# Two attention blocks in fp32: layer 0's V by Strassen twice over in all seven products, and the softmax sums inside it in two parts

## The chip, the cores and the metric

The kernel runs on one core of one Trainium2 chip. The metric is the time of one execution on the device in microseconds; lower is better. A core has TensorE (PE, matrix products), VectorE (DVE), ScalarE (ACT), GpSimd (POOL) and SyncE (SP), each with a stream of instructions of its own that it takes in order. SP and ACT also issue the DMAs here.

## The reference, cut to what matters

Eight samples of 512 channels by 1024 positions go through two attention blocks, everything in fp32.

```python
def _L0_conv_ref(x, norm_w, norm_b, qkv_w, qkv_b, proj_w, proj_b):   # 8 heads of 64 channels
    h = group_norm(x, norm_w, norm_b)
    qkv = jnp.einsum('oc,bchw->bohw', qkv_w, h) + qkv_b[None, :, None, None]
    ...
    attn = jax.nn.softmax(jnp.einsum('bhnd,bhmd->bhnm', q, k) * scale, axis=-1)
    o = jnp.einsum('bhnm,bhmd->bhnd', attn, v)
    ...
    return x + jnp.einsum('oc,bchw->bohw', proj_w, o) + proj_b[None, :, None, None]

def _L1_conv_ref(x, gn_gamma, gn_beta, wq, bq, wk, bk, wv, bv, wo, bo):   # one head of 512 channels
    ...
```

The change is in V of layer 0: a 512x512 weight times 512 channels by 1024 positions, for one sample.

## The kernel before, in words

**Strassen.** Each such product is cut 2x2 and made as seven products instead of eight: of the weight's parts `A11, A12, A22, S1` to `S4` and the sample's parts `B11, B21, B22, T1` to `T4`. `S` and `T` are sums and differences of quarters. The seven are kept in `PAIRS` (A12 B21, S1 T1, S4 B22, A22 T4) and `REST` (A11 B11, S2 T2, S3 T3). A "second step" makes each of the seven again by seven smaller ones. `make_twice` makes the weight's smaller sums once, in sample 0's attention, and stores them in DRAM; `WeightTwice` loads them from ACT's queue; `quarters_in_steps` makes the sample's, three DVE instructions for each part.

**Samples and stages.** While sample b is in layer 0's attention, nothing of b + 1 but its norm and its parts is made. Then `middle` makes, in this order: V of sample b + 1, the first half of its Q and K (the QK stage), the projection of sample b, and the second half of Q and K. Layer 1 of sample b follows, then attention of b + 1. `Kept` stores V, Q and K in DRAM meanwhile. There are seven such middles. Sample 0's own V is made in another way (`make_v`).

**V before.** `make_v_twice` calls `by_two_steps`: the four products of `PAIRS` by a second step (generator `pair`, two products side by side in a PSUM bank, each small product two matmuls of 128 columns), then the three of `REST` in one step (generator `line`, matmuls of 256 columns). Seven small products use two banks in turn: `line`, in which A11 B11, S2 T2, S3 T3 and A22 T4 are added up and read off after each, and `single`. Each is read off by ACT (`nc.scalar.copy`, the first to write a place) or by DVE (an add onto it).

**Banks.** Tags `s` and `o` have two PSUM buffers each of two banks, taken in turn. A group's `line` is an `s`, its `single` an `o`. So a stage's first products wait until the same buffers of the stage before are read off. `spares` holds the unused second banks, and `room(name, n)` gives the n-th.

**Softmax sums inside V.** The last two pairs of heads (the last "couple") end with attention. `fold` moves half of their sums over keys by DMA, `folded` adds them on DVE, `sum_couple` adds over partitions on PE with `ones` (eight matmuls of 64 rows by 32 columns), `copy_couple` copies to SBUF on ACT, and the rest is a chain of DMAs and one reciprocal:

```python
def one_over_couple(couple, queues):
    nc.vector.reciprocal(few, few)
    ...
    nc.sync.dma_start(rows.rearrange("m (a c) -> (m a) c", c=32), few)      # inv_rows <- few
    ...
            queues[j].dma_start(flat(spreads[pair])[j * HD : (j + 1) * HD], ...)   # inv <- inv_rows
```

In V `queues` are SP and ACT. `held_couple` is a short ACT instruction on `few`; `divide_at` (DVE) divides the attention's output `o` by the sums in the QK stage, and POOL halves the result for the projection.

**The order.** It is written out by hand: a generator yields after each small product, and `at_steps` runs the hooks of step n after it. `combine2` (T1 to T4 of `o`, on DVE), the fold, the sums and loads are such hooks in V. In attention, `ahead_steps` and `at_units` do the same by units; a unit is 1.716 us of PE (four score and four value matmuls). SBUF tiles come from one pool of 36 buffers (`tile2`), so that a new tile may wait for an old one.

**Where seven products by two steps stand already.** Layer 1's Q (`make_q_twice`) uses `seven_by_two_steps`: four groups z (A11 B11 and S2 T2), w (S3 T3 alone), c (S1 T1, A22 T4) and d (A12 B21, S4 B22), interleaved, first "zzwzwzwzwzwzww", then "ccdcdcdcdcdc", `exchange(0)`, "d", "d", `exchange(1)`.

Of the kernel before, what the change touches and what calls it, by code (L numbers as in the profile page):

```python
# [39 lines left out]
ALU = mybir.AluOpType  # L40
# [25 lines left out]
def two_attention_blocks(  # L66
# [488 lines left out]
    PAIRS_Q = [[("A12", "B21"), ("S4", "B22")], [("S1", "T1"), ("A22", "T4")]]  # L555
    PAIRS = [[("A12", "B21"), ("S1", "T1")], [("S4", "B22"), ("A22", "T4")]]
    REST = [[("A11", "B11"), ("S2", "T2")], [("S3", "T3")]]
    TWICE = {"wqk1": PAIRS + REST}

    class WeightTwice:  # L560

# [120 lines left out]
        yield from together(pair(0), pair(1))  # L682
        yield from together(line(0), line(1))

    def seven_by_two_steps(multiply, at, z, c, w, bias, name):

        def group(tag, products, use_of):
            line, single = (banks(t, f"ps_{t}{tag}_{name}") for t in "so")
            spares.extend([single[:, 1, :], line[:, 1, :]])
            line, single = line[:, 0, :], single[:, 0, :]
            for bank, x, y, start, fresh, r, t in [
                (line, "A11", "B11", True, True, 0, 0), (single, "A12", "B21", True, False, 0, 0),
                (line, "S2", "T2", False, True, 0, 1), (single, "S1", "T1", True, True, 1, 1),  # L700
                (line, "S3", "T3", False, False, 1, 1), (single, "S4", "B22", False, False, 0, 1),
                (line, "A22", "T4", False, True, 1, 0),
            ]:
# [24 lines left out]
        for k in range(2):  # L728
            plus(z[k][:, 1, :], z[k][:, 0, :], z[k][:, 1, :], bias and bias(k, 0))
        for k in range(2):  # L730
            plus(w[k], w[k], z[k][:, 1, :], bias and bias(k, 1))
        spares.clear()
        c_of, d_of = [("S1", "T1"), ("A22", "T4")], [("A12", "B21"), ("S4", "B22")]
        second = dict(c=group("c", c_of, (c, False)), d=group("d", d_of, (z, True)))

        def exchange(k):
            plus(z[k][:, 1, :], z[k][:, 1, :], c[k][:, 0, :])
            both = w[k].unsqueeze(1).to_broadcast([P, 2, HALF])
            nc.gpsimd.tensor_tensor(c[k], c[k], both, ALU.add)
# [266 lines left out]
    class Kept:  # L1006


        def __init__(self, pairs, name):
            self.name, self.n = name, [len(p) for p in pairs]  # L1010
            tiles = [flat(t) for p in pairs for t in p]
            self.rows = dram.tile([P, len(tiles) * N], FP, tag=f"kept_{name}", name=f"kept_{name}")
            for n, t in enumerate(tiles):
                nc.sync.dma_start(self.rows[:, n * N : (n + 1) * N], t)

        def back(self):
            n, pairs = 0, []
            for size in self.n:
                pairs.append([])
                for _ in range(size):  # L1020
                    pairs[-1].append(tile2(f"{self.name}_back_{n}"))
                    nc.sync.dma_start(flat(pairs[-1][-1]), self.rows[:, n * N : (n + 1) * N])
                    n += 1
            return pairs

    def pairs_qk_twice(w, twice_a, oc, bs, twice_b, pairs, b):

# [128 lines left out]
    def layer0(bs, qs, ks, vs, b, norm_next, ending, begun):  # L1156
# [69 lines left out]
        if b == 0:  # L1226
# [16 lines left out]
            hooks[7].append(p0.finish)  # L1243
            at_steps(together(*pairs_qk(w, 1, bs, qs, ks, b)), hooks)
            steps = []
            for name, ns in [("v0", range(2)), ("p0", range(2)), ("wqk1", range(4))]:
                of = [columns_of(of) for of in waiting if of.name == name]
                steps += make_twice(name, ns, of[0] if of else None, early=not of)
            for n, step in enumerate(steps):
# [50 lines left out]

        couples, folds, ps_couple = [ORDER[:2], ORDER[2:]], {}, []

        def fold(pair):

# [12 lines left out]
        def sum_couple(couple, banks_of):  # L1319


            for n, (pair, j) in enumerate((pair, j) for pair in couple for j in range(2)):
                for g, bank in enumerate(banks_of):
                    rows = slice(g * HD, (g + 1) * HD)
                    nc.tensor.matmul(
                        bank[n * 32 : (n + 1) * 32, :], ones[rows, :32], accs[pair, 0][rows, j, :],
                        start=True, stop=True,
                    )
            ps_couple[:] = banks_of

        def copy_couple(couple, g):
            if g == 0:
# [34 lines left out]
        def couple_steps(i):  # L1367
            if ended(i - 1) is not None:
                fold(ended(i - 1))
            if ended(i - 5) is not None:  # L1370
                folded(ended(i - 5))
            couple = couples[0]
            if ended(i - 7) == couple[1]:
                ps_sum = banks("o", f"ps_sum_{b}_{couple[0]}")
                sum_couple(couple, [ps_sum[:, g, :] for g in range(2)])
# [8 lines left out]
        ahead_a, ahead_b, ahead = [], {}, {}  # L1384

        def ahead_steps(i):
            if i == 44:
                for part in ["B21", "T1", "B22", "T4"]:
                    ahead_b[part], steps = quarters_in_steps(
                        combine.parts[part], tile2(f"{part}_twice_0_{b + 1}_0")  # L1390
                    )
                    for step in steps:
                        ahead[45 + len(ahead)] = step
# [112 lines left out]
    def middle(b, bs, twice_w, twice_b, comb, combine2, bias, hooks_v, divisions):  # L1506
# [1 line left out]


        to, comb_twice, xs = {"qs": [None] * NC, "ks": [None] * NC}, {}, []  # L1510
        v_pairs = places_v(f"0_{b + 1}")
        hooks_v.setdefault(8, []).append(lambda: twice_w.append(WeightTwice("qk02")))
        at_steps(
            make_v_twice(next_weight("v0"), twice_w.pop(0), bs, twice_b, v_pairs, f"v_0_{b + 1}"), hooks_v
        )
# [6 lines left out]
        hooks = {n: [division] for n, division in enumerate(divisions)}  # L1522
        for n in range(1, 5):
            hooks[2 * n + 3] = [lambda n=n: combine2(n, 1)]
        for n, part in [(3, "B21"), (3, "B22"), (5, "T1"), (11, "T4")]:
# [1161 lines left out]
```

## Time and profile before

| what | value |
|---|---|
| time, median of 3 runs | 2778.61 us (2778.32 to 2780.92) |
| the profiled execution's own time | 2779.2 us |
| its span in the profile | 2777.5 us |
| one V stage, first product to QK's first | 24.24 us, in each of the seven |
| QK stage after it | 22.39 us |
| attention of layer 0 (samples 0 to 6) | 110.35 us |
| granted TensorE clock | full throughout |

"Busy" on PE runs from a matmul's start to its modelled end; matmuls overlap, so the pace is read from start to start. An fp32 matmul leaves two records. "Idle before, releaser" names what ended an engine's idle time. In lists by order of time the columns are start, duration (both us), engine, line, operation, output and inputs, shapes, count.

### The profile page before, as it was taken

How to read it: one execution, taken by the hardware profiler on the slowest of the kernel's cores; microseconds unless marked ns; L12 is line 12 of the kernel's file. 1: busy time of each engine (PE TensorE's matmuls, PEld its weight loads, DVE VectorE, ACT ScalarE, POOL GpSimd, SP SyncE). 2: the span in 40 equal slices, each digit the busy share in tenths (PEclk: the TensorE clock that was granted, in tenths of full speed). 3: DMA queues.
4: the chain of work that ended last, by engine and by line, in shares of the span. 5: the costliest groups of instructions: out<-in, count | busy, mean ns of one | idle time of the engine just before them, and what ended most of it. 6: DMA issues, size and time to landing. Idle time of an engine off the chain costs nothing.

```text
span 2777.5 us, 41752 instructions
## 1 busy us (share of the span) xinstructions
PE 2769.1 (100%) x16318; PEld 1646.7 (59%) x16318; DVE 2137.0 (77%) x3023; ACT 1186.8 (43%) x1911; POOL 589.4 (21%) x612
## 2 busy tenths in 40 slices
PE   9999999999999999999999999999999999999999
PEld 5437764377643786447764477645676356853375
DVE  6797777877778777887778776887768877688877
ACT  3462533625346153462525525265342643226621
POOL 0001440015400253002530044300432005220121
PEclk9999999999999999999999999999999999999999
DMA  7545514265142652326432263322633236241101
GB/s 257 202 135 199 200 57 141 59 210 184 57 141 59 213 182 80 122 62 231 156 120 82 77 227 145 136 74 73 239 129 140 69 101 239 71 171 32 35 16 40
DMA packets 114527, 358.62 MB, mean 129 GB/s; under 512 B 25052, under 2 KB 25852, under 8 KB 107920
## 3 DMA queue, kind: packets, MB, share of 16 engines
q1 hardware_dynamic: 89856, 299.68, 31.6%
q10 hardware_dynamic: 24464, 56.16, 6.2%
q8 instruction: 131, 2.15, 0.3%
q14 instruction: 76, 0.62, 0.1%
HBM read 252.77 MB, written 79.21 MB: 120 GB/s over the span
## 4 chain that ended last, share of the span: by engine, by line
PE 96%; DVE 2%; DMA 1%; ACT 1%; issue 0%; SPq 0%; POOL 0%; ACTq 0%; POOLq 0%
PE ps_o L1195 16%; PE s L1146 16%; PE ps_o L2005 10%; PE ps_l_qk L1044 5%; PE ps_l L1837 5%; PE ps_l_v L793 5%; PE ps_s L1820 4%; PE ps_s L1837 4%; PE ps_s_qk L1037 3%; PE ps_s_v L1065 3%; PE ps_o_qk L1037 3%; PE ps_l_p L778 3%; PE ps_o_v L1065 2%; PE ps_s_two L2135 2%; PE ps_s_p L1102 2%; PE ps_o_two L2135 1%
## 5 line engine op out<-in xcount | busy, mean ns | idle before, releaser
L950 ACT ACTIVATE p<-s 128x1024 f32<-128x1024 f32 x505 | 516.4, 1024 | 308.6 <-PE s L1146 301.1
L952 DVE TENSOR_TENSOR acc<-acc,p 128x1024 f32<-128x1024 f32 x384 | 468.6, 1220 | 63.6 <-ACT p L950 54.9
L1146 PE MATMUL s<-qk_back,qk_back 64*64 64x512 f32 x3528 | 457.4, 590 | 0.0
L1195 PE MATMUL ps_o<-p,v_back 64*64 64x512 f32 x3528 | 455.3, 589 | 0.0
L1195 PEld LDWEIGHTS ps_o<-p,v_back 64*64 64x64 f32 x3528 | 134.9, 133 | 243.6 <-issue 239.8
L1146 PEld LDWEIGHTS s<-qk_back,qk_back 64*64 64x64 f32 x3528 | 132.6, 133 | 245.5 <-issue 216.4
L537 POOL TENSOR_TENSOR B_twice_p<-o 128x512 f32<-128x512 f32 x14 | 20.9, 1492 | 1065.8 <-DVE o L1215 1065.8
L2005 PE MATMUL ps_o<-t_p,s_v 128*128 128x512 f32 x384 | 169.6, 596 | 0.0
L1811 ACT ACTIVATE p<-p,factor 128x512 f32<-128x512 f32 (+1 forms) x112 | 84.5, 780 | 113.3 <-DVE p L1847 86.3
L1847 DVE TENSOR_TENSOR p<-ps_l,p 128x512 f32<-128x512 f32 x136 | 91.5, 687 | 44.9 <-PE ps_l L1837 43.2
L2005 PEld LDWEIGHTS ps_o<-t_p,s_v 128*128 128x128 f32 x384 | 71.8, 190 | 88.4 <-issue 88.0
L1825 ACT COPY p<-ps_s 128x512 f32<-128x512 f32 x96 | 53.1, 588 | 166.3 <-PE ps_s L1820 166.3
L665 DVE TENSOR_TENSOR c_v<-ps_l_v,c_v 128x512 f32<-128x512 f32 x120 | 80.0, 687 | 54.4 <-PE ps_l_v L793 54.2
L537 POOL TENSOR_TENSOR B_twice<-x 128x512 f32<-128x512 f32 x23 | 38.3, 1667 | 358.6 <-DVE x L1457 177.2
L952 DVE TENSOR_TENSOR acc<-p,p 128x1024 f32<-128x1024 f32 x57 | 69.6, 1222 | 48.4 <-ACT p L950 48.4
L1847 DVE TENSOR_TENSOR p<-ps_s,p 128x512 f32<-128x512 f32 x112 | 74.8, 685 | 31.4 <-PE ps_s L1837 29.7
L1044 PE MATMUL ps_l_qk<-t,w_qk 128*128 128x512 f32 x224 | 98.7, 592 | 0.0
L647 ACT COPY c_q<-ps_s_qk 128x512 f32<-128x512 f32 x56 | 32.6, 583 | 139.1 <-PE ps_s_qk L1037 139.1
L647 ACT COPY c_v<-ps_s_v 128x512 f32<-128x512 f32 x90 | 52.7, 585 | 91.1 <-PE ps_s_v L1065 91.1
L1808 POOL TENSOR_TENSOR acc<-acc,p 128x512 f32<-128x512 f32 x48 | 83.5, 1740 | 13.3 <-ACT p L1811 10.8
L1044 PEld LDWEIGHTS ps_l_qk<-t,w_qk 128*128 128x128 f32 x224 | 42.5, 190 | 54.0 <-issue 53.1
L667 DVE SCALAR_TENSOR_TENSOR c_q<-ps_l_qk,vec,c_q 128x512 f32<-128x512 f32 x56 | 40.8, 749 | 39.7 <-PE ps_l_qk L1044 39.7
(693 smaller groups left out, 5762.6 us busy)
## 6 DMA issues: line engine op xcount, KB each, us to landing
x<-in_x SPq DMA_DIRECT2D x64, 512.0 KB, 9.3
qk_back<-kept_qk SPq DMA_DIRECT2D x56, 512.0 KB, 6.5
w_qk<-stored_qk SPq DMA_DIRECT2D x14, 1792.0 KB
fold<-acc SPq DMA_DIRECT2D x56, 256.0 KB, 3.0
qk_twice<-stored_qk_twice ACTq DMA_DIRECT2D x28, 512.0 KB, 4.9
kept_v<-c_v SPq DMA_DIRECT2D x28, 512.0 KB, 5.1
kept_qk<-c_q SPq DMA_DIRECT2D x28, 512.0 KB, 2.6
kept_qk<-c_k SPq DMA_DIRECT2D x28, 512.0 KB, 3.5
```

Of the source, the lines that this page charges most:

```text
L793: nc.tensor.matmul(bank[:, u * 2 * P : (u + 1) * 2 * P], bs[b][:, k, n * P : (n + 1) * P], w[a][:, k, :], start=fresh and u == k == 0, sto ...
L950: nc.scalar.activation(p, s, AF.Exp, scale=factor)
L952: nc.vector.tensor_tensor(acc, first, p, ALU.add)
L1037: nc.tensor.matmul(bank[:, i * 2 * P : (i + 1) * 2 * P], parts[a][x], twice_b[v][y], start=start and i == 0, stop=True, skip_group_check=True,
L1044: nc.tensor.matmul(bank, of(i, a)[:, k, :], bs[v][:, k, :], start=start and k == 0, stop=k == 1, skip_group_check=True,)
L1065: nc.tensor.matmul(bank[:, (2 * i + u) * P : (2 * i + u + 1) * P], twice_b[v][y][:, u * P : (u + 1) * P], parts[a][x], start=start and i = ...
L1146: nc.tensor.matmul(s[cols, j, :], ks[pair][k0 // HALF][rows, k0 % HALF : k0 % HALF + HD], qs[pair][g][rows, :], start=True, stop=True,)
L1195: nc.tensor.matmul(o[cols, half, :], vs[n][kt % 4 // 2][rows, h, c0 : c0 + HD], p[rows, j, :], start=kt == 0, stop=kt == NT - 1,)
L1820: nc.tensor.matmul(bank, bs[v][:, k, t * P : (t + 1) * P], of[a][k], start=a == "A11" and k == 0, stop=k == 1, skip_group_check=True,)
L1837: nc.tensor.matmul(bank[:, u * 2 * P : (u + 1) * 2 * P], v[y][:, u * P : (u + 1) * P], a[x], start=start and u == 0, stop=True, skip_group ...
L1847: nc.vector.tensor_tensor(at(r, t), bank, at(r, t), ALU.add)
L2005: nc.tensor.matmul(bank, v_parts[kt // 2][a][:, kt % 2, c * P : (c + 1) * P], p_parts[kt // 2][b][:, kt % 2, cols], start=fresh and kt == ...
```

## The change

V of the next sample in `middle` is made by `make_v_all`, which uses `seven_by_two_steps`: all seven products take the second step. For it, `make_twice` makes the weight's sums of seven products instead of four, B11, T2 and T3 are halved in attention's units 35 to 43, and `WeightTwice("v0")` loads four tiles (three and a half full) instead of two. The wide add of `exchange` is on DVE in V (`engine`), on POOL as before in layer 1's Q. V lies in two z and two c tiles; `Kept` stores it in eight DMAs of half a tile.

The sums over partitions are made in two parts, each for one half of the rows (g), each in the same spare bank, after steps 16 and 20 of 28, where all of it was after step 12 of 20. `combine2` moves from step 3 to 4, the fold from 6 to 9, `one_over_couple` from 14 to 23, `held_couple` from 16 to 26, the load of QK's weights from 8 to 11. In QK the four divides move one step later, from steps 0 to 3 to 1 to 4.

```diff
-    TWICE = {"wqk1": PAIRS + REST}
+    TWICE = {"wqk1": PAIRS + REST, "v0": PAIRS + REST}
...
-    def seven_by_two_steps(multiply, at, z, c, w, bias, name):
+    def seven_by_two_steps(multiply, at, z, c, w, bias, name, engine=nc.gpsimd):
...
             both = w[k].unsqueeze(1).to_broadcast([P, 2, HALF])
-            nc.gpsimd.tensor_tensor(c[k], c[k], both, ALU.add)
+            engine.tensor_tensor(c[k], c[k], both, ALU.add)
...
+    def make_v_all(w, twice_a, twice_b, name):
+        parts = twice_a.all(columns_of(w))
+        def multiply(bank, products, x, y, start):
+            for i, (a, v) in enumerate(products):
+                for u in range(2):
+                    nc.tensor.matmul(
+                        bank[:, (2 * i + u) * P : (2 * i + u + 1) * P],
+                        twice_b[v][y][:, u * P : (u + 1) * P], parts[a][x],
+                        start=start and i == u == 0, stop=True, skip_group_check=True,
+                    )
+        def at(tiles, r, t):
+            both = tiles[t] if len(tiles[t].shape) == 2 else flat(tiles[t])
+            return both.rearrange("p (m o) -> p m o", o=2 * P)[:, :, r * P : (r + 1) * P]
+        z, c = ([tile2(f"{n}_{name}_{t}") for t in range(2)] for n in "zc")
+        w_of = tile2(f"w_{name}")
+        u = [w_of[:, k, :] for k in range(2)]
+        pairs = [[[z[t][:, n, :], c[t][:, n, :]] for t in range(2)] for n in range(2)]
+        return pairs, seven_by_two_steps(multiply, at, z, c, u, None, name, nc.vector)
...
-            for name, ns in [("v0", range(2)), ("p0", range(2)), ("wqk1", range(4))]:
+            for name, ns in [("v0", range(4)), ("p0", range(2)), ("wqk1", range(4))]:
...
-            if i == 44:
-                for part in ["B21", "T1", "B22", "T4"]:
+            for at, parts in [(34, ["B11", "T2", "T3"]), (44, ["B21", "T1", "B22", "T4"])]:
...
-                    3: [lambda n=n: combine2(n, 0) for n in range(1, 5)],
-                    6: [lambda: folded(end)],
-                    12: [
-                        lambda: sum_couple(couples[1], [room("sum", g) for g in range(2)]),
-                        lambda: copy_couple(couples[1], 0), lambda: copy_couple(couples[1], 1), gather_couple,
+                    4: [lambda n=n: combine2(n, 0) for n in range(1, 5)],
+                    9: [lambda: folded(end)],
+                    16: [lambda: sum_couple(couples[1], {0: room("sum", 2)}), lambda: copy_couple(couples[1], 0)],
+                    20: [
+                        lambda: sum_couple(couples[1], {1: room("sum", 2)}),
+                        lambda: copy_couple(couples[1], 1), gather_couple,
                     ],
-                    14: [lambda: one_over_couple(couples[1], [nc.sync, nc.scalar])],
-                    16: [held_couple],
+                    23: [lambda: one_over_couple(couples[1], [nc.sync, nc.scalar])],
+                    26: [held_couple],
```

More of the change, by code (lines that the diff above doesn't have):

```diff
@@ L1010, in __init__ @@
             self.name, self.n = name, [len(p) for p in pairs]
-            tiles = [flat(t) for p in pairs for t in p]
+            tiles = [t for p in pairs for t in p]
             self.rows = dram.tile([P, len(tiles) * N], FP, tag=f"kept_{name}", name=f"kept_{name}")
             for n, t in enumerate(tiles):
-                nc.sync.dma_start(self.rows[:, n * N : (n + 1) * N], t)
+                parts = t if isinstance(t, list) else [flat(t)]
+                size = N // len(parts)
+                for k, part in enumerate(parts):
+                    nc.sync.dma_start(self.rows[:, n * N + k * size : n * N + (k + 1) * size], part)
         def back(self):
@@ L1299, in divide_both @@
                 divide(pair, g, spreads[pair][:, g, :])
-        couples, folds, ps_couple = [ORDER[:2], ORDER[2:]], {}, []
+        couples, folds, ps_couple = [ORDER[:2], ORDER[2:]], {}, {}
         def fold(pair):
@@ L1322, in sum_couple @@
             for n, (pair, j) in enumerate((pair, j) for pair in couple for j in range(2)):
-                for g, bank in enumerate(banks_of):
+                for g, bank in banks_of.items():
                     rows = slice(g * HD, (g + 1) * HD)
@@ L1328, in sum_couple @@
                     )
-            ps_couple[:] = banks_of
+            ps_couple.update(banks_of)
         def copy_couple(couple, g):
@@ L1374, in couple_steps @@
                 ps_sum = banks("o", f"ps_sum_{b}_{couple[0]}")
-                sum_couple(couple, [ps_sum[:, g, :] for g in range(2)])
+                sum_couple(couple, {g: ps_sum[:, g, :] for g in range(2)})
             for at, step in [
@@ L1386, in ahead_steps @@
         def ahead_steps(i):
-            if i == 44:
-                for part in ["B21", "T1", "B22", "T4"]:
+            for at, parts in [(34, ["B11", "T2", "T3"]), (44, ["B21", "T1", "B22", "T4"])]:
+                if i != at:
+                    continue
+                for n, part in enumerate(parts):
                     ahead_b[part], steps = quarters_in_steps(
@@ L1391, in ahead_steps @@
                     )
-                    for step in steps:
-                        ahead[45 + len(ahead)] = step
+                    for k, step in enumerate(steps):
+                        ahead[at + 1 + 3 * n + k] = step
             if i == 54:
@@ L1510, in middle @@
         to, comb_twice, xs = {"qs": [None] * NC, "ks": [None] * NC}, {}, []
[L1511 to L1515, printed above, removed]
+        hooks_v.setdefault(11, []).append(lambda: twice_w.append(WeightTwice("qk02")))
+        v_pairs, steps = make_v_all(next_weight("v0"), twice_w.pop(0), twice_b, f"v_0_{b + 1}")
+        at_steps(steps, hooks_v)
         to["v"] = Kept(v_pairs, f"v_{b % 2}")
@@ L1521, in middle @@
         pairs = places_qk(0, b + 1)
-        hooks = {n: [division] for n, division in enumerate(divisions)}
+        hooks = {n + 1: [division] for n, division in enumerate(divisions)}
         for n in range(1, 5):
-            hooks[2 * n + 3] = [lambda n=n: combine2(n, 1)]
-        for n, part in [(3, "B21"), (3, "B22"), (5, "T1"), (11, "T4")]:
+            hooks.setdefault(2 * n + 3, []).append(lambda n=n: combine2(n, 1))
+        for n, part in [(4, "B21"), (4, "B22"), (5, "T1"), (11, "T4")]:
             hooks[n].append(lambda part=part: halve(part))
```

## The prediction

> **What bounds the kernel now.** I read the page's busy times first, then its chain of work that ended last, then the busy times by stage, then the instructions in order of time in one V stage.
>
> ```profile
> PE 2769.1 (100%) x16318; PEld 1646.7 (59%) x16318; DVE 2137.0 (77%) x3023; ACT 1186.8 (43%) x1911; POOL 589.4 (21%) x612
> PE 96%; DVE 2%; DMA 1%; ACT 1%; issue 0%; SPq 0%; POOL 0%; ACTq 0%; POOLq 0%
> ```
>
> PE is the whole path: a PE instruction saved is time saved, and a wait put in front of PE is time lost. Busy times by stage (microseconds, then PE, PEld, DVE, ACT, POOL) of layer 0's attention for sample 2, its V stage, and attention for sample 0:
>
> ```profile
> 452.10:562.40 110.30, 110.30 (x1033) 38.71 (x1032) 94.20 (x101) 72.26 (x82) 0.00 (x0) 1.00 0.26 73
> 562.40:586.70 24.30, 24.30 (x181) 22.09 (x178) 14.02 (x21) 6.74 (x15) 0.00 (x0) 1.00 0.42 110
> 110.80:221.10 110.30, 110.30 (x1033) 38.84 (x1032) 101.66 (x162) 69.23 (x76) 0.00 (x0) 1.00 0.41 127
> ```
>
> DVE has 16.1 us free in attention, but only 8.6 us in sample 0's. PE in sample 2's V stage (start, duration, count):
>
> ```profile
> 562.41 0.71 PE L1065 MATMUL ps_s_v<-w_v,x 128*128 128x128 f32 x4
> 562.96 0.61 PE L1065 MATMUL ps_s_v<-w_v,t 128*128 128x128 f32 x4
> ...
> 573.68 0.61 PE L1065 MATMUL ps_s_v<-w_v,T_twice 128*128 128x128 f32 x4
> 574.22 1.09 PE L1325 MATMUL ps_o_v<-acc,ones 64*32 64x512 f32 x16
> 575.24 0.71 PE L1065 MATMUL ps_s_v<-w_v,B_twice 128*128 128x128 f32 x4
> 575.79 0.61 PE L1065 MATMUL ps_s_v<-w_v,T_twice 128*128 128x128 f32 x4
> 576.24 3.67 PE L793 MATMUL ps_l_v<-w_v,x 128*128 128x256 f32 x16
> 579.75 7.07 PE L793 MATMUL ps_l_v<-w_v,t 128*128 128x256 f32 x32
> 586.65 0.59 PE L1037 MATMUL ps_s_qk<-x,w_qk 128*128 128x256 f32 x2
> ```
>
> The starts give the pace, not the durations, which overlap. A row of x4 is one small product (two matmuls, two records each); the next one starts 0.447 us later (mean over the rows shown and left out). The three one-step products take 3.51 + 6.90 = 10.41 us. The sums cost 575.79 - 573.68 - 2 x 0.447 = 1.22 us. The stage lasts 24.24 us, with no gap. Last, ACT's and the DMA queues' part of the same stage:
>
> ```profile
> 578.83 0.34 DVE L1345 RECIPROCAL few<-few 128x32 f32<-128x32 f32 x1
> 579.20 0.34 SPq L1347 DMA_DIRECT2D inv_rows<-few  x1
> 580.65 1.13 ACTq L1351 DMA_DIRECT2D inv<-inv_rows  x2
> 581.83 0.23 ACT L960 ACTIVATE held_inv<-few 128x32 f32<-128x32 f32 x1 [4.64 <-issue]
> ```
>
> held_inv needs only the reciprocal, done at 579.17, yet starts at 581.83: ACT waited for inv_rows to land (1.45 us after its issue) and then issued two DMAs (1.13 us). Whatever stands behind those DMAs on ACT is held 2.66 us. Here that costs nothing: no copy is behind them.
>
> **What the Trainium skill says.** "TensorEngine Tiling (Array Packing)", Tiling Modes: 64x32 splits the array into 8 independent tiles. The trace agrees: 16 records (8 matmuls, two passes) take 1.09 us. "VectorE: DVE Perf Modes", the TRN2 errata section: fp32 tensor_tensor takes (N+151)/0.96 ns; that is 691 and 1224, and the trace has 687 to 690 and 1220. "DMA: Bandwidth & Descriptors", Anatomy of one DMA: a semaphore wait before a DMA happens on the issuing sequencer; held_inv above shows it.
>
> **The change, part by part**, per sample (seven have it). Times are from the V stage's start.
>
> *Products.* 28 small products and 10.41 us become 7 x 7 = 49 small ones: 21 x 0.447 = 9.39 us for 10.41. **-1.02 us.**
>
> *Sums in two parts.* Each half runs 4 matmuls on one half of the rows, the other half of the array idle. A pass streams the same 512 columns, so I take 1.22 us for each half (bounds: 0.6, were time by matmuls, to 1.3). **+1.22 us**; PE's own stage is then 24.44 us.
>
> *DVE in the first half.* In the program's order DVE has: o add (done 1.45, as now), z and w adds, T1 to T4 (2.53 us in the trace), two z adds, the fold add (1.22), and only then the add that empties w's `line` bank. w<-ow ends at 4.36 (its product ends at 3.67, plus 0.27 to DVE's start), T1 to T4 at 6.81, the z adds at 7.42 and 8.21, fold at 9.34, w at 9.68. PE wants that bank for w's last product at 9.03. **+0.69 us** (0 to 1).
>
> *ACT's wait now has work behind it.* PE resumes after the second half of the sums at 18.08 (without the 0.69, which I add at the end). ACT copies it by 18.98, few is issued at 19.01; the reciprocal comes after step 23's add, at 21.74; inv_rows at 22.11; ACT's two inv DMAs from 23.54 (+1.43) to 24.71. Behind them on ACT stands the copy of c's last product (step 25, done 22.65): 24.76 to 25.35. It frees c's `line` bank, the one QK's first product takes. That was due at 24.44: **+0.99 us** (0 if ACT doesn't block, 1.5 if few lands late).
>
> *DVE at the end.* Of `exchange(0)`, the plus reads c[0], which that copy writes (in V, `at` picks the tile by t; in layer 1's Q, by r, so there it doesn't), and its 1024-wide add is now on DVE instead of POOL. Both stand ahead of the adds of d's last two products. So plus 25.45, wide add 26.05 to 27.27 (1.22 by the acc row and the price above; a broadcast operand isn't shown), z adds to 27.88 and 28.48. QK's second product takes d's `line` bank: it starts at 28.55 instead of 26.30. **+2.25 us** (1.35 if ACT's copy is on time: the wide add alone does that).
>
> *After that.* exchange(1) ends at 30.2, when inv, issued near 24, should have landed (median 4.5 us, most 6.7): the divides go between QK's adds; QK's bank o0 is free at 31.4 and wanted at 32.9. Nothing more there; at the worst 2 us. The eight kept_v DMAs for four, the 1.79 MB of weights for 1.05 (four ACT issues for two, about 0.8 us more where ACT is 35% idle) and the x loads behind them have slack: x is wanted at the projection, 22.4 us after. If that slack is gone, PE waits there.
>
> Sum: -1.02 + 1.22 + 0.69 + 0.99 + 2.25 = **+4.13 us a sample, +28.9 us for seven.**
>
> *DVE in attention.* B11, T2, T3 are halved there: 3 x (0.60 + 2 x 0.34) = 3.8 us in units 35 to 43. In samples 1 to 6 the gaps between DVE's instructions in that stretch (508 to 525 us, in order of time) are 5.7 us: nothing. In sample 0 three weight sums (3 x 0.93 us) come too and push wqk1's ten units later, onto the halvings. Adding up DVE's instructions in the new order, unit 54's acc ends at 212.3 instead of 208.9. The new tiles use up the pool: by the program's waits, the exponential of unit 57 (208.41 now) then needs that add. Its p, ready at 213.35, is wanted by PE at 210.3: 3.0 us, and about 1.2 us of DVE's backlog shows in that V stage. **+4.2 us once** (0 to 6).
>
> The profiled execution took 2779.2 us (span 2777.5), 0.6 above the median 2778.61. 2779.2 + 28.9 + 4.2 = 2812.3; against the median I say **2812**.
>
> **The rivals.**
> A. *ACT's block is avoided or smaller*: step 25's copy gets through in time. The terms are -1.02 + 1.22 + 0.69 + 0 + 1.35 = 2.24; x 7 + 4.2 = 19.9: 2799. For it: where few lands soon the chain has no slack to lose. Against: held_inv.
> B. *Faster*: the waits don't decide. One mechanism: the adds on DVE and copies on ACT keep up with PE, as in layer 1's Q stage, which runs the same seven products in 21.7 us with POOL doing the wide add; and the half sums cost 0.6 each. Then -1.02 x 7 = -7.1: 2771.5. It decides if d's last add is done before 0.86 us into QK, 3.2 us sooner than I have it; DVE's order doesn't allow it.
> C. *Nothing to measure*: only the sums and sample 0's load cost, 0.2 x 7 + 4.2 = 5.6, at the edge: 2784 or less.
> D. *Worse*: inv lands late behind the 1.8 MB w_qk load that follows, DVE sits at the divide with QK's adds behind it, and 1 to 2 us more go in each sample: 2822.
> That the change doesn't do what it says is excluded by the order of the instructions: 98 small matmuls, no one-step ones.
>
> **Numbers.** Mine 0.55 (2805 to 2818 alone), A 0.21, D 0.13, B 0.06, C 0.05. Range 2797 to 2823. About 0.2%, 5.6 us, is what a measurement of this kernel tells from no change: faster 0.06, same 0.05, slower 0.89.
>
> **What would show it.** V's small products at 0.447; two rows of L1351's sums, x8 each, still near 1.1 us; a PE gap of 0.7 before w's last product; ACT's copy of c after the two inv DMAs; QK's second product starting some 3 us late behind DVE; V to QK 28.4 us instead of 24.24; the first sample's attention some 3 us longer, the others 110.35. If QK's second product follows its first by 0.86 us, I am wrong; if the half sums take 0.6, by 8.5 us.

## The result and the profile after

The changed kernel takes 2830.02 us (median of 3 runs, 2827.38 to 2830.2) for 2778.61: ratio 1.0179, 95% interval 1.0165 to 1.0193. It is slower by 51.4 us, where the prediction said 33 and at most 44. The profiled execution took 2827.38 us, span 2825.7, 48.2 more than the span before.

The page's busy times and its chain of the work that ended last:

```profile
PE 2788.6 (99%) x16570; PEld 1656.7 (59%) x16570; DVE 2199.7 (78%) x3154; ACT 1197.5 (42%) x1939; POOL 587.7 (21%) x612
PE 92%; DVE 4%; DMA 1%; issue 1%; ACT 1%; ACTq 0%; SPq 0%; POOL 0%; DVEq 0%; POOLq 0%
```

PE was 96% of the chain and is 92%: other engines now hold it up. PE's busy time grew by 19.5 us, where the prediction's products and sums make 7 x 0.2 = 1.4; that is the first hint that its instructions themselves got longer. The busy times of the same three stages as before (an attention, the V stage after it, sample 0's attention; columns as in the prediction, then the granted clock, DMA share and GB/s). The prediction calls the first sample 2's; by the count of stages it is sample 1's, and only the V made after it is sample 2's:

```profile
463.20:573.50 110.30, 110.30 (x1033) 38.71 (x1032) 97.80 (x110) 72.27 (x82) 0.00 (x0) 1.00 0.28 80
573.50:599.50 26.00, 24.82 (x216) 22.50 (x212) 15.39 (x25) 8.06 (x18) 0.00 (x0) 1.00 0.24 69
110.40:229.10 118.70, 113.59 (x1034) 39.04 (x1033) 107.82 (x183) 68.99 (x76) 0.00 (x0) 0.99 0.43 131
```

Samples 1 to 6 hide the halvings in attention, as predicted. By stage, from the first product's start to that of the next stage (in order of time):

| stage | before | after | change in all |
|---|---|---|---|
| attention, sample 0 | 110.35 | 118.69 | +8.3 |
| V, seven | 24.24 each | 26.01 to 26.81, sum 183.65 | +14.0 |
| QK, seven | 22.39 each | 24.95 (three), 26.26, 27.26, 27.65, 27.78 | +27.1 |
| all other stages | | | -1.2 |

The view of waits, PE's rows, says which waits make it up (us in all, times, longest):

```profile
PE ps_s_qk L1063 <- DVE z_v L711: 14.4, 7, 2.1
PE ps_s_qk L1063 <- ACT c_v L709: 6.5, 7, 1.5
PE s L1172 <- ACT p L950: 5.1, 2, 3.4
PE ps_sw_v L1036 <- DVE w_v L711: 3.2, 7, 0.5
```

The first, second and fourth are the three waits per sample that the prediction named, in their places; the third is sample 0's attention. They make 29.2 us, and 48.2 are to be explained. PE in the stages that make V and Q, K of sample 2, in order of time:

```profile
582.11 0.61 PE L1036 MATMUL ps_ow_v<-v_twice,t 128*128 128x128 f32 x4
583.18 0.71 PE L1036 MATMUL ps_sw_v<-w_v,T_twice 128*128 128x128 f32 x4 [0.46 <-DVE w_v L711]
...
585.51 1.06 PE L1036 MATMUL ps_sd_v<-w_v,x 128*128 128x128 f32 x8
586.50 1.06 PE L1351 MATMUL ps_od_v<-acc,ones 64*32 64x512 f32 x8
587.49 1.16 PE L1036 MATMUL ps_sc_v<-v_twice,T_twice 128*128 128x128 f32 x8
588.49 1.06 PE L1036 MATMUL ps_od_v<-w_v,x 128*128 128x128 f32 x8
...
599.52 0.70 PE L1063 MATMUL ps_s_qk<-x,w_qk 128*128 128x256 f32 x2 [0.74 <-ACT c_v L709]
600.06 0.59 PE L1063 MATMUL ps_s_qk<-t,w_qk 128*128 128x256 f32 x2
602.71 1.22 PE L1063 MATMUL ps_s_qk<-x,w_qk 128*128 128x256 f32 x2 [2.05 <-DVE z_v L711]
603.72 1.06 PE L1063 MATMUL ps_s_qk<-t,w_qk 128*128 128x256 f32 x2
604.58 1.06 PE L1063 MATMUL ps_o_qk<-x,w_qk 128*128 128x256 f32 x2
```

Half of the sums costs 588.49 - 585.51 - 2 x 0.895 = 1.19 us, by the measure that gave 1.22 for the whole in the prediction (a row of x8 here is two small products, 0.895). After the wait of 2.05 us comes what the prediction had not foreseen: a row that takes 0.43 us from start to start elsewhere (605.58 to 606.01 in e3b below) takes 0.86 (603.72 to 604.58). The windows of this stretch give the reason in the column after PE's busy time, the granted clock:

```profile
600.00:601.00 1.00, 0.66 (x4) 1.00 1.04 238
601.00:602.00 1.00, 0.00 (x0) 0.83 1.02 234
602.00:604.00 2.00, 1.29 (x3) 0.50 1.13 242
...
608.00:610.00 2.00, 2.00 (x10) 0.88 1.00 382
```

While PE waits, its clock falls to half, at 601.66, and stays there for 6.8 us, of which 5.8 lie after the wait. The other three long QK stages show the same, for 6.8, 3.4 and 6.8 us; the three of 24.95 us show none.

"TensorE: Matmul & The Clock Gate" in the Trainium skill (Part 1) describes such a gate: half rate after an idle window of about 3.4 us that runs freely, full rate after a busy one. The trace agrees in the half, in the length (the clock's record has 3.41 or 6.83 us) and in the free running: the changes in after's record lie whole multiples of 3.413 us apart. But the window need not be idle throughout. The stages of samples 2 and 5 have the same two waits, 0.74 and 2.05 us. On the grid of 3.413 us the windows with the most idle time in these two stages are:

```profile
598.25:601.66 3.41, 1.66 (x9) 1.00 0.80 210
1639.32:1642.73 3.41, 2.00 (x12) 1.00 0.70 185
```

After the first, in which PE was busy for 1.66 of 3.41 us, the clock is half; after the second, 2.00 us, it stays full. So it goes in all seven stages: half after 1.13, 1.13, 1.66 and 1.66 us of busy time, full after 1.89, 1.98 and 2.00. With equal waits, where they happen to fall on the grid decides which sample loses its clock. (Laid over all the runs here, the grid shows no loss where PE idled less than 1.69 us of a window, and a loss wherever it idled more than 1.90; in between both occur.)

### The profile page after: what moved, and what is told of

Read it like the earlier page. It is cut to its first block, busy times and chain, and to the rows that moved or that the text cites. A ratio compares the mean times of both kernels' runs of the same rounds, so it can differ in the third digit from the quotient of the medians.

```text
span 2825.7 us, 42535 instructions
## 1 busy us (share of the span) xinstructions
PE 2788.6 (99%) x16570; PEld 1656.7 (59%) x16570; DVE 2199.7 (78%) x3154; ACT 1197.5 (42%) x1939; POOL 587.7 (21%) x612
## 4 chain that ended last, share of the span: by engine, by line
PE 92%; DVE 4%; DMA 1%; issue 1%; ACT 1%; ACTq 0%; SPq 0%; POOL 0%; DVEq 0%; POOLq 0%
PE ps_o L1221 15%; PE s L1172 15%; PE ps_o L2032 10%; PE ps_l_qk L1070 5%; PE ps_l L1864 5%; PE ps_s L1847 4%; PE ps_s L1864 4%; PE ps_s_qk L1063 3%; PE ps_o_qk L1063 3%; PE ps_l_p L778 3%; PE ps_l_v L793 2%; PE ps_s_two L2162 2%; PE ps_s_p L1128 2%; PE ps_o_two L2162 1%; PE ps_s_v L1091 1%; PE ps_o_p L1128 1%
## 5 line engine op out<-in xcount | busy, mean ns | idle before, releaser
L1172 PE MATMUL s<-q,k 64*64 64x512 f32 x512 | 67.5, 599 | 5.1 <-ACT p L950 5.1
L373 POOL TENSOR_TENSOR rstd<-rstd,minus_half 128x4 f32<-128x4 f32 (+1 forms) x16 | 12.9, 806 | 273.0 <-DVE rstd L372 273.0
L667 DVE SCALAR_TENSOR_TENSOR c_q<-ps_l_qk,vec,c_q 128x512 f32<-128x512 f32 x56 | 40.7, 748 | 36.8 <-PE ps_l_qk L1070 36.7
```

The lines of the kernel that those rows point to most:

```text
L1172: nc.tensor.matmul(s[cols, j, :], ks[pair][k0 // HALF][rows, k0 % HALF : k0 % HALF + HD], qs[pair][g][rows, :], start=True, stop=True,)
```

## The experiments

Theory: three waits, each in front of PE, and a clock that their idle time halves; in sample 0 the tile pool behind a full DVE. The rivals stand with each run. The table has the medians, and the stages of each profiled execution (attention is sample 0's; V and QK are single stages, smallest to largest):

| run | median us | ratio to before (95%) | attention | V | QK |
|---|---|---|---|---|---|
| before | 2778.6 to 2779.9 | 1 | 110.35 | 24.24 | 22.39 |
| after | 2830.02 | 1.0179 (1.0165 to 1.0193) | 118.7 | 26.01 to 26.81 | 24.95 to 27.78 |
| e1_sp | 2806.72 | 1.0096 (1.0079 to 1.0113) | 120.1 | 25.10 to 25.41 | 24.01 to 24.89 |
| e2_exlate | 2812.92 | 1.0117 (1.0100 to 1.0134) | 119.8 | 26.05 to 26.36 | 23.81 to 24.62 |
| e3_fill | 2824.20 | 1.0162 (1.0145 to 1.0179) | 119.3 | 26.01 to 26.12 | 25.92 |
| e3b_fill2 | 2820.38 | 1.0145 (1.0128 to 1.0162) | 120.3 | 26.01 to 27.25 | 24.95 to 24.96 |
| e4_pool0 | 2831.37 | 1.0193 (1.0176 to 1.0210) | 123.3 | 26.01 to 26.78 | 24.95 to 27.71 |
| e6_both | 2809.78 | 1.0109 (1.0092 to 1.0126) | 119.7 | 25.10 | 24.76 to 25.25 |
| e6s_onesum | 2808.18 | 1.0101 (1.0084 to 1.0118) | 119.1 | 24.80 | 24.76 to 24.97 |
| e8_place0 | 2827.67 | 1.0177 (1.0160 to 1.0194) | 112.4 | 26.02 to 27.14 | 26.24 to 27.86 |
| e9_best | 2808.40 | 1.0105 (1.0088 to 1.0122) | 112.6 | 24.12 | 25.96 to 26.97 |
| e10_late | 2829.66 | 1.0178 (1.0161 to 1.0195) | 112.4 | 23.83 to 23.84 | 28.30 to 30.64 |
| e11_place_dve | 2824.43 | 1.0168 (1.0151 to 1.0185) | 110.35 | 23.83 to 23.84 | 28.30 to 29.37 |
| e12_last | 2796.16 | 1.0063 (1.0049 to 1.0076) | 110.3 | 23.83 | 24.79 to 26.49 |

### The clock: idle matmuls in the wait (e3, e3b)

```diff
+        def fill():
+            bank = room("fill")
+            for _ in range(4):          # 2 in e3b
+                nc.tensor.matmul(bank, bs["B11"][:, 0, :P], bs["B11"][:, 0, :], start=True, stop=True)
+        hooks[0] = [fill]
```

> After QK's first product PE makes four matmuls more, 128x512 in fp32, that nobody reads (about 1.72 us of a 2.05 us wait); nothing else changes, so every wait of after stays. Theory (idle time on PE halves the granted clock for some us): the QK stages run at full clock, the four long ones get as short as the other three (24.95 us): 9.2 us faster, 2821. Rival (the clock falls for another reason, or what slows these products is DMA traffic): no change, 2830; or, if the extra work only delays PE, slower.

> As e3, with two idle matmuls after QK's first product instead of four. In e3's trace one takes 0.86 us, not 0.43 as its text had it, so that four (3.4 us) outlast the wait of 2.05 us by about 1 us (QK 25.92 in all seven, none at half clock); two are 1.72 us, inside the wait. Theory (PE's idle time halves the clock): QK 24.95 in all seven, no half clock there; in all 183.8 us of QK in after become 174.7: 2821. Rival (only full occupation, without any gap, keeps the clock): some QK stages stay at 26 to 27.8 us, 2825 to 2830.

e3 takes 2824.2 us: more work, and 5.8 us less time than after, though four idle matmuls (3.4 us) outlast the wait and each QK is 25.92. e3b keeps inside the wait; its PE, the same place in sample 2:

```profile
602.83 1.88 PE L1554 MATMUL ps_o_qk<-x 128*128 128x512 f32 x4
605.04 0.70 PE L1063 MATMUL ps_s_qk<-x,w_qk 128*128 128x256 f32 x2 [0.34 <-DVE z_v L711]
605.58 0.59 PE L1063 MATMUL ps_s_qk<-t,w_qk 128*128 128x256 f32 x2
606.01 0.59 PE L1063 MATMUL ps_o_qk<-x,w_qk 128*128 128x256 f32 x2
```

The wait ends when it did (3.19 us after QK's first product), the products after it are back at 0.43, and all seven QK stages take 24.95 or 24.96. Their sum falls from 183.80 to 174.70, 9.1 us as expected; the kernel from 2830.02 to 2820.38. Nothing about the waits was touched, so the theory's clock is shown: PE's idle time costs these 9 us on top of itself.

### ACT's DMAs (e1)

```diff
-                    23: [lambda: one_over_couple(couples[1], [nc.sync, nc.scalar])],
+                    23: [lambda: one_over_couple(couples[1], [nc.sync, nc.sync])],
```

> All four inv DMAs are issued by SP, none by ACT; all else as after (2830.0). Theory (waits, and TensorE's clock halved by the idle time they leave): the copy of c's last product no longer stands behind ACT's DMAs. QK's first product loses its wait (0.74 to 1.54 us in the trace of after, 6.5 in all), its second product waits 1.35 instead of 2.05 to 2.2 us, about 6 in all, and as PE never idles for 2 us the clock stays full, another 9 us: 2808. Rival 1 (the clock falls for another reason than PE's idle time): 2817. Rival 2 (inv comes about 1.2 us later from one queue and the divides, with QK's adds behind them, wait for it): 2815 to 2820, with DVE idle before the first divide.

2806.72 for an expected 2808: 23 us less than after, by one word. V falls by 0.91 and stops varying but for one stage, QK to 24.01 to 24.03 in six of seven, without half clock. Its rows of the waits (PE):

```profile
PE ps_s_qk L1063 <- DVE z_v L711: 8.5, 7, 1.2
PE s L1172 <- ACT p L950: 5.8, 2, 3.9
```

The wait for ACT's copy is gone, and the wait for DVE fell from 2.05 to 1.2 us, which is the exchange alone. The QK stages keep the clock: no window of the grid there has more than 1.21 us of idle time. Inv comes from one queue now, and in six of seven QK stages DVE does not wait for it; in the seventh, the one of 24.89 us, it waits 0.80 us. Rival 2 is out as the general case. In after ACT stood like this (start, duration):

```profile
597.66 1.13 ACTq L1377 DMA_DIRECT2D inv<-inv_rows  x2
598.89 0.58 ACT L709 COPY c_v<-ps_sc_v 128x512 f32<-128x512 f32 x1 [5.79 <-PE ps_sd_v L1036]
```

The copy's product had ended by 597.0; it waits for inv_rows to land (issued 596.22, 1.44 us) and for the two issues (1.13 us), as the prediction worked out. In two other samples the chain was later (inv's issues started 2.23 us after that of inv_rows in one, and took 1.59 us in the other), which made V 26.81 and 26.47.

### exchange(0) behind d's adds (e2), and both (e6)

```diff
-        exchange(0)
         yield from in_order("d", **second)
         next(second["d"])
+        exchange(0)
         exchange(1)
```

(for V alone; layer 1's Q keeps its order.)

> exchange(0) comes after the adds of d's last two products instead of before them; ACT still issues two inv DMAs. Theory: d's banks come free at once, QK's second product follows its first by 0.86 us (3.19 after); 7 x 2.3 = 16 us and the 9 us of half clock in the QK stages go: 2805; QK's first product still waits 0.75 to 1.5 us for ACT. Rival (late inv: the divides now meet PE 2.3 us earlier, inv lands some 6.5 us after its issue, and QK's bank o0 waits for an add behind the divide): 1 us a sample comes back, 2812, with a PE wait for c_q's add in front of o0.

> Both edits of e1 and e2: SP issues all four inv DMAs, and exchange(0) comes after the adds of d's last two products. Theory (two separate waits at the end of V): V stays at e1's 25.10 us, QK goes from e1's 24.01 to 22.7 to 23.4 us (its second product no longer waits 1.2 us; DVE's queue of plus, wide adds and divides costs 0.3 to 1 us later in QK), the clock stays full: e1's 2806.7 less 4 to 9, 2798 to 2802. Rival (the divides then wait for inv, with QK's adds behind them): QK at 24 us or more, 2806.

e2: 2812.92 for 2805 expected. QK's second product is on time, as the theory says, and no QK is at half clock, but QK is 23.8, where 24.95 less 2.3 would be 22.65. e6 is worse than e1 (2809.78 for 2798 to 2802): V is e1's 25.10, QK rose to 24.76. The number is the rival's, its reason is not. DVE in e6 from d's last add on, in order of time:

```profile
256.33 0.69 DVE L711 TENSOR_TENSOR z_v<-ps_sd_v,z_v 128x512 f32<-128x512 f32 x1 [0.20 <-PE ps_sd_v L1039]
257.13 0.69 DVE L716 TENSOR_TENSOR z_v<-z_v,c_v 128x512 f32<-128x512 f32 x1
257.85 1.23 DVE L739 TENSOR_TENSOR c_v<-c_v,w_v 128x1024 f32<-128x1024 f32 x1
259.00 0.69 DVE L716 TENSOR_TENSOR z_v<-z_v,c_v 128x512 f32<-128x512 f32 x1
259.72 1.23 DVE L739 TENSOR_TENSOR c_v<-c_v,w_v 128x1024 f32<-128x1024 f32 x1
260.86 0.68 DVE L1244 TENSOR_TENSOR o<-o,inv 128x512 f32<-128x512 f32 x1
261.46 0.68 DVE L644 TENSOR_TENSOR c_q<-ps_o_qk,c_q 128x512 f32<-128x512 f32 x1
```

There is no idle time: it is not inv (only one of the seven QK stages, the one of 25.25 us, has a wait for inv, 0.39 us). The two exchanges (3.7 us) and the divides stand ahead of QK's adds (L644), whose bank PE wants back. The work that no longer holds QK's second product holds its seventh.

### The sums in one part (e6s)

```diff
-                    16: [lambda: sum_couple(couples[1], {0: room("sum", 2)}), lambda: copy_couple(couples[1], 0)],
                     20: [
-                        lambda: sum_couple(couples[1], {1: room("sum", 2)}),
-                        lambda: copy_couple(couples[1], 1), gather_couple,
+                        lambda: sum_couple(couples[1], {g: room("sum", 2 + g) for g in range(2)}),
+                        lambda: copy_couple(couples[1], 0), lambda: copy_couple(couples[1], 1), gather_couple,
```

> As e6_both, with the sums over partitions in one part after step 20 (both halves, in two spare banks) instead of two parts after steps 16 and 20. The trace of after has the first product after each half 0.99 us after the half's start, before's whole had 1.22. Theory (a half costs 0.99): V 0.76 us shorter, 24.3, 5.3 us less than e6_both. Rival (a half costs as much as the whole, as the prediction had it): V 1.22 us shorter, 8.5 us less. Rival 2 (a half costs half, and the split is free): V the same.

V falls by 0.30, between the theory's 0.76 and nothing. The theory compared unlike things: 0.99 us is from the start of a half to the next product, and by that measure the whole took 1.02 before (574.22 to 575.24), not 1.22. By the prediction's measure a half is 1.19 and the whole 1.22, so the two halves cost 2.38, 1.16 more than the whole did before.

The single part did not run at 1.22 in these versions. In e9, which has the same sums, it costs 2.07 by the same measure: the first sum starts at 239.52 in bank od, and the first in bank sd only at 240.38, 0.06 us after DVE's add from the bank beside it ended at 240.32 (239.63 + 0.69). The two banks belong to one buffer of two banks, and the sums wait as if they were one. 2.38 - 2.07 = 0.31 is the gain in V. With two spare banks of the tag o (e10 to e12) that wait is gone, but now the product in bank od waits for ACT's copy of the sums beside it (0.32 us in e12's trace): 1.79 in all, and V is another 0.29 shorter. No version ran the single part unhindered; the split's price of 1.16 rests on the traces of before and after.

### Sample 0's attention (e4, e8, and e11 below)

```diff
e4 and e8: halvings of B11, T2, T3 on POOL for sample 0
+                        nc.gpsimd if b == 0 and at == 34 else nc.vector,
e4: V's added weight sums on POOL, in their place
-            for name, ns in [("v0", range(4)), ("p0", range(2)), ("wqk1", range(4))]:
+            for name, ns, engine in [
+                ("v0", range(2), nc.vector), ("v0", range(2, 4), nc.gpsimd),
...
e8: on POOL, and in units of their own
-            for name, ns in [("v0", range(4)), ("p0", range(2)), ("wqk1", range(4))]:
+            for name, ns in [("v0", range(2)), ("p0", range(2)), ("wqk1", range(4))]:
...
+                    rest = make_twice(name, range(2, 4), of[0], nc.gpsimd)
...
+                at_units.setdefault(10 + 2 * n, []).append(step)
```

> In sample 0's attention alone, POOL instead of DVE makes the halvings of B11, T2 and T3 and the weight sums of V's A11, S2 and S3 (POOL is idle there); the tiles and their order stay. Theory (DVE's overload, some 6.6 us of added instructions, makes the exponentials wait): sample 0's attention is back from 118.69 to 110.4 us, 8.3 us faster, 2821.7; the half clock in it goes too, since there is no idle time. Rival (it is the number of tiles: the pool makes the exponentials wait for transfers and weight sums whoever makes them): a gap of 1.7 us or more stays, 2825 to 2830.

> After, with the work of sample 0's attention moved: V's weight sums of A11, S2 and S3 on POOL in units 10 to 18, beside those on DVE, so that the projection's and wqk1's sums stand in the same units as before; the halvings of B11, T2, T3 on POOL. Unlike e4, the weight sums of wqk1 are no longer ten units late. Theory (the exponentials waited because wqk1's tiles came free late, behind a DVE that is full at the end): attention of sample 0 back to 110.4 to 112 us, 2830 - 8 = 2822. Rival (the three more tiles of the pool suffice for the wait): 118 us, 2830.

In after two waits stand in this stage (PE in order of time):

```profile
201.70 1.04 PE L1221 MATMUL ps_o<-p,c_v 64*64 64x512 f32 x8
204.44 1.09 PE L1172 MATMUL s<-q,k 64*64 64x512 f32 x8 [1.70 <-ACT p L950]
...
214.20 1.04 PE L1221 MATMUL ps_o<-p,c_v 64*64 64x512 f32 x8
218.65 1.32 PE L1172 MATMUL s<-q,k 64*64 64x512 f32 x8 [3.41 <-ACT p L950]
219.72 1.95 PE L1221 MATMUL ps_o<-p,c_v 64*64 64x512 f32 x8
221.43 1.72 PE L1172 MATMUL s<-q,k 64*64 64x512 f32 x8
```

and ACT's exponentials before them waited for these:

```profile
203.36 1.94 ACT L950 ACTIVATE p<-s 128x1024 f32<-128x1024 f32 x2 [3.82 <-DMA acc<-acc]
...
217.57 1.94 ACT L950 ACTIVATE p<-s 128x1024 f32<-128x1024 f32 x2 [3.86 <-DVE wqk_twice L520]
```

The first gap costs 1.9 us, the second 3.6 (start to start, less 0.86), half clock after it about 1.7, smaller waits the rest of 8.3. As the releasers read, both exponentials want a tile of the pool: one that the fold's transfer had last, one that wqk1's weight sum had last. e4 takes 6.6 us of instructions off DVE and is worse, 123.3. e8 puts wqk1's sums back to their old units: 112.4, no wait of an exponential left. The place of wqk1's sums matters, then; e11 below tells it from the amount, as e8 also takes work off DVE. (e8's total falls by 2.4 only: in its profile more of the seven middles are at half clock, QK's sum is 3.0 us up, V's 1.0.)

What POOL costs DVE, from DVE and POOL in e8 at the same time:

```profile
165.66 0.82 DVE L520 TENSOR_TENSOR wqk_twice<-again_wqk 128x128 f32<-128x128 f32 x1
...
167.21 0.28 DVE L520 TENSOR_TENSOR wqk_twice<-again_wqk 128x128 f32<-128x128 f32 x1
...
169.35 1.05 DVE L520 TENSOR_TENSOR wqk_twice<-again_wqk 128x128 f32<-128x128 f32 x1
```

```profile
164.74 2.40 POOL L543 TENSOR_TENSOR B_twice<-x,B_twice 128x256 f32<-128x256 f32 x2
168.97 1.28 POOL L537 TENSOR_TENSOR T_twice<-t 128x512 f32<-128x512 f32 x1 [1.83 <-DVE acc L952]
```

A 0.28 us add takes 0.82 or 1.05 while POOL works. "SBUF — State Buffer" in the Trainium skill (SBUF: two separate sides) has a port pair that a DVE instruction with two SBUF inputs and a POOL instruction that reads SBUF take in turn, each for its whole length. The trace agrees, down to the exception: adds with one input in PSUM (L644) stay at 0.68 beside POOL in e12.

### All together (e9), and DVE's work in QK placed elsewhere (e10, e11, e12)

e9 adds to e6s the fold after step 14 instead of 9, both wide adds on POOL, and e8's sample 0.

> All together: SP issues the inv DMAs; exchange(0) after d's last adds, both wide adds on POOL; the sums in one part; the fold's add after step 14 instead of 9 (behind w's adds); sample 0's work placed as in e8. Theory: V = 49 x 0.447 + 1.22 + 0.2 = 23.3 us with no gap, QK 22.4 to 22.7, sample 0's attention 110.4 to 112: 45.8 for 46.63 in each of seven, 2778.6 - 6 + 0 to 1.7 = 2773 to 2775, the first version faster than before. Rival (POOL's wide adds, 2.4 us each, or the late fold's sums hold PE): a wait of 0.5 us or more in V or QK, 2778 to 2785.

V is 24.12 for e6s's 24.80: with the late fold no wait for w's bank is left. QK is 26 to 27, so the total is e1's again, 2808.4. DVE in its first QK:

```profile
252.02 0.79 DVE L1244 TENSOR_TENSOR o<-o,inv 128x512 f32<-128x512 f32 x1 [1.97 <-DMA inv<-inv_rows]
252.74 0.68 DVE L644 TENSOR_TENSOR c_q<-ps_o_qk,c_q 128x512 f32<-128x512 f32 x1
253.34 2.23 DVE L1244 TENSOR_TENSOR o<-o,inv 128x512 f32<-128x512 f32 x1
```

Now that DVE comes to the divide early, it does wait for inv, 1.97 us here and 1.7 to 2.9 in all seven QK stages, with QK's adds behind it (the prediction's rival D), and the next divide takes 2.23 for 0.68 beside POOL's wide add.

The next three move DVE's work in QK by its hooks:

- e10: exchange(0) after QK's step 3, divides after 5 to 8, exchange(1) after 9, T1 to T4 after 10 to 13; the sums in two banks of the tag o.
- e11: the same, with sample 0's added work on DVE (`rest` without `nc.gpsimd`).
- e12: as e11, but exchange(0) in V's end, exchange(1) after QK's step 3, divides after 4 to 7, T's after 6, 7, 8, 13.

> As e9, but both exchanges and the four divides go into the QK stage where DVE has room: exchange(0) after QK's step 3, the divides after 5 to 8, exchange(1) after 9, all on DVE; V's stores after step 10, x's loads after 11, T1 to T4 of the projection after 10 to 13. The sums use two spare banks of the tag o. Theory (in e9 QK's adds stood behind divides that waited for inv, and DVE ran at half pace beside POOL's wide adds): QK back to 22.4 to 22.7, V 23.4 to 24.1, sample 0's attention 112.4: 2779 - 0 to 6 + 2 = 2775 to 2781. Rival (the projection now waits for T4, for POOL's halvings or for x): the projection's stage over 22.39, 2785.

> As e10, with nothing of sample 0's added work on POOL: V's added weight sums are on DVE in units 10 to 18, the halvings on DVE, the projection's and wqk1's sums in the units of before. Theory (what cost sample 0's attention 8.3 us is that wqk1's sums came ten units later, into DVE's full end, not the amount added; and POOL slows DVE when both run, 0.82 us for a 0.28 us add in e8): attention 110.4 to 112, like e10 or up to 2 us faster. Rival (the 6.6 us more on DVE count wherever they stand): 115 us or more, 3 us or more slower than e10.

> As e11, with DVE's work in QK spread otherwise: exchange(0) in V after d's last adds (as e6), exchange(1) after QK's step 3, the divides after steps 4 to 7, T1, T2 and T4 of the projection after 6, 7 and 8, T3 after 13, POOL's halvings from 8 on, V's stores after 4, x's loads after 8. Theory (e10 and e11 filled DVE between QK's steps 8 and 14 so that its adds came 3 to 5 us late for the line products; inv lands some 4.3 us into QK, and DVE must do the divides between that and the adds of step 8): QK 22.4 to 23.0, V 23.83, attention 110.35: 46.2 to 46.8 for 46.63 in each of seven, 2776 to 2781. Rival (DVE is too full in QK for exchange(1) and the divides in any order once V takes all seven products by two steps): QK 24 us or more, 2789 or more.

e11 against e10 settles sample 0: with nothing on POOL and all added work on DVE, but wqk1 in its old units, attention is 110.35 as before the change. It is the place, not the amount, and not the number of tiles; POOL's help cost 2.0 us (112.4 in e10). In QK both failed, 28.3 to 30.6: in e10 PE waits 31.8 us in all for DVE's instructions (L667, L644) ahead of the line products. e12 is the best changed version, 2796.16, yet its QK is 24.8, mostly by one wait, 1.6 of 2.4 us (PE's rows of the waits):

```profile
PE ps_s_qk L1068 <- DVE c_k L644: 11.3, 7, 1.6
PE ps_od_v L1041 <- ACT sums L965: 2.2, 7, 0.3
```

Its account closes: V -0.41 x 7 = -2.9, QK +18.6 (one of the seven at half clock), attention 0: +15.7, for 14.8 between the spans of the two profiled executions (the medians are 16.7 apart). None of the versions beats the kernel before. In the windows DVE was busy 18.6 of QK's 22.4 us before the change, so 3.7 us of exchange leave next to nothing. Whether an order of V's groups that ends the c group earlier would find DVE's room inside V was not tried.

## Why the prediction was right or wrong

Right: the direction, the names and places of the waits, and nearly all that it said of V and QK's first products. By its own times QK's second product would start 28.55 + 0.69 = 29.24 us after V's first; in sample 2 it does after 29.19. At full clock V and QK together are 4.33 us longer a sample, for 4.13 forecast. Wrong: the sum, by 15 us of 48 in the profile. The measured column adds up to 48.1 (the medians are 51.4 apart; the profiled execution was the fastest of the three).

| term | forecast, us | measured | by |
|---|---|---|---|
| products, sums, w's bank, ACT (V) | +1.88 x 7 | +1.77 x 7 | V's stages, smallest |
| of it: products | -1.02 | -1.02 | 49 x 0.447 |
| of it: sums in two parts | +1.22 | 2 x 1.19 for 1.22: +1.16 | V in order of time |
| of it: w's bank behind the fold | +0.69 | +0.73 | in order of time; e9 |
| of it: ACT's DMAs ahead of c's copy | +0.99 | +0.91 | e1 |
| late inv chain in two samples, a pause in the last V | 0 | +1.6 in all | V's stages over 26.01 |
| QK's second product behind DVE | +2.25 x 7 | +2.56 x 7 | QK stages at full clock |
| half clock after PE's idle time, QK | 0 | +9.1 in all | e3b |
| sample 0's attention | +3.0, and 1.2 in its V | +8.3, and 0 | order of time; e11 |
| other stages | 0 | -1.2 | what is left of 48.2 |

*The step that failed first* is a term put at nothing: "Nothing more there; at the worst 2 us." A stage with a PE wait was priced by the wait alone. Measured, 9.1 us came after the waits in four of the seven QK stages, at half clock. The granted clock, shown at full throughout before, was read as given; e3b shows that it hangs on PE's idle time.

*The second* is "Its p, ready at 213.35, is wanted by PE at 210.3: 3.0 us". The wait that it names is there, and on time: in after an exponential waits for DVE's acc and its p is ready at 213.23, but PE's next matmuls start at 213.29, 0.88 us after those before them, where 0.86 is the pace. The waits that count came earlier and later, at the tiles that the fold's transfer and wqk1's sums held: 8.3 us in this stage. "Push wqk1's ten units later, onto the halvings" had the cause, but followed it only for DVE's time, not for the tiles of those sums. Half clock made it worse here too.

Smaller: late inv chains in two samples (1.3 us) and a pause of 0.3 us in the last V had no term, and QK lost 0.31 us a sample more than forecast. The half of the sums was rightly taken as long as the whole. The sign "V to QK 28.4 us" was a slip: it books all 4.13 us on V, but 2.25 of them stand behind QK's first product, which by the prediction's own times comes at 26.12 (measured 26.01). The gaps of DVE from 508 to 525 us are 5.1 us in the trace, not 5.7; the 3.8 us of halvings still fit.

Rival D (late inv) did not decide after's time: its DVE never idled for inv in the QK stages. It appeared once the other waits were gone (e9). Rival A's case is e1's edit: without ACT's block 2806.7, for A's 2799; most of the difference is sample 0's 9.7 us for 4.2. Rival B asked DVE to be done with d's last add 3.2 us sooner. With exchange(0) behind it (e2, e6) it is, but then QK's later products wait; none of the orders tried brought the gain.

## What to carry to other kernels

Price an added wait on a busy TensorE by the wait plus what the clock may lose after it: here that hung on how much of one clock window of 3.4 us was idle, about half of it being the limit, and so in part on where the wait fell. Look at the granted clock's windows in the changed trace before looking for a further wait; useless matmuls in the gap are a cheap test. Before a cost is compared between two traces, measure it the same way in both: 0.99 against 1.22 looked like a gain and was 1.19 against 1.22. When work moves to an engine that is 83% busy in the next stage, write out its queue there too: taking the wait in front away moved it to the next bank three times here. When steps are inserted in a hand-written order, what costs is often what they push later, so give them places of their own.

## What was not expected of the hardware

- The clock fell to half though no gap on PE was longer than 2.05 us, in four of seven stages with nearly the same waits, and came back after 3.41 or 6.83 us. In these stages it followed windows of 3.413 us in which PE was busy for 1.66 us or less, not those with 1.89 or more. With one wait of 1.2 us (e1) the QK stages kept full clock; with 1.6 us (e12) one of seven lost it.
- POOL holds DVE up: DVE adds with both inputs in SBUF took 0.82 to 1.05 us for 0.28, and 2.23 for 0.68, beside POOL; adds from PSUM kept 0.68.
- In this program two PSUM banks of one buffer wait as one: sums in one bank started 0.06 us after DVE's last read of the other. The wait is the program's own; that the banks as such need it is not shown.
- Four matmuls of 64x32 on half of the rows (eight records) cost 1.19 us, all eight 1.22.
